# Output projection of a decoder layer: one Strassen scheme against two, one inside the other

## Chip, cores and metric

One Trainium2 chip, one of its cores. The metric is the device time of the whole kernel in microseconds (us). The kernel computes in fp32, with bf16 for the quantised cross attention and a split into two halves for the down projection.

## The reference, cut to what matters

Two batch entries of 512 tokens and 1024 features pass one decoder layer: self attention with a window of 128, a cross attention of quantised products, and a gated feed-forward, each followed by a layer norm.

```python
q = (x @ wq.T).reshape(B, N, N_Q, HD)...        # 32 heads of 128
k = (x @ wk.T)...; v = (x @ wv.T)...            # 8 heads of 128, each for 4 query heads
o = _gqa_swa_attention(q, k, v, SLIDE)
o = o.transpose(0, 2, 1, 3).reshape(B, N, N_Q * HD)
return o @ wo.T                                  # the output projection: 512 x 4096 by 4096 x 1024
...
x = _layernorm(x + _L0_attn_ref(x, L0_attn_wq, L0_attn_wk, L0_attn_wv, L0_attn_wo), axis=-1)
x = _layernorm(x + _L0_xattn_ref(x, ctx_4096, ...), axis=-1)
x = _layernorm(x + _L0_ffn_ref(x, L0_ffn_w_gate, L0_ffn_w_up, L0_ffn_w_down), axis=-1)
```

## The kernel before

The large products use Strassen's scheme: a product of two by two blocks is made from seven block products in place of eight, with sums of blocks formed beforehand on each side and sums of products formed afterwards.

Attention (`attention`) runs over 16 groups: batch entry `b` 0 and 1, and within each the 8 key heads `g`. For each group the queries, keys and values are projected (`project`, which calls `strassen`, line L113 for its matmuls): three calls with seven products each, a product being four matmuls of 128x256. For each of the four query tiles `i` of a group, `scores` multiplies queries by keys (L306) into `ps`, two PSUM banks; ACT copies the parts of the window to `s` (L318 to L322), VectorE lays the masked diagonal over them (L323), and the softmax follows. `weigh` transposes the weights (`pt`, L343) and multiplies by the values (`o`, L366 to L369), with a PSUM bank of its own. After the last tile `keep` (L379 on) forms the Strassen left sums of the group, four VectorE operations on 512 columns, and writes seven factors to `kept` in DRAM with five DMAs.

`project_out` multiplies these by the weights `wo`. One level of Strassen: for each of two token parts `q`, the seven products `k` in the order 1, 6, 2, 7, 5, 4, 3, and for each the 8 groups `s`. A step loads one left factor (128 KB) and one right factor (512 KB), three steps ahead, and issues two matmuls of 128x512 (L465). Products 2, 7, 4 and 3 go on accumulating in the banks of earlier ones. After the last group of a product, VectorE adds it to the residual `x` (L472). The sums of the right side are formed once, during attention, by `sum_output_weights` (L938 to L941), and lie in `wo_sums`.

`Cross` holds the cross attention: `context` quantises the context, `tokens` handles one tile of 128 tokens after another. `feed_forward` runs 22 units per batch entry, 21 of them a Strassen product of gate and up weights, and sums two or four units at a time in the down projection (`down`, L719).

Nothing of this runs one after the other. `Background` holds generators, and each call of `between` from the attention loop (six per query tile) or after each product of the feed-forward takes a step of them. `behind` holds the context of the first entry, then `output(0)`, then `output(1)`; `aside` holds the tokens of the cross attention; `ahead` holds the weight sums. `output(0)` starts with the second entry's attention. `output(1)` starts when the tokens of entry 0 are done, and runs mostly under the feed-forward of entry 0. A scheduler then sets the order of the instructions on each engine, save where `keep_in_program_order` holds one in place; each engine runs its own in order.

PSUM has eight banks. In attention: two for `ps_p` (Strassen and the cross attention), two for `ps_y` (the output of entry 0; Strassen uses them too as long as `b` is 0), two for the scores, one for transposes and one for `o`. In the feed-forward: two for `ps_p` (the output of entry 1 and the cross attention), four for Strassen (`ps_gu`, `ps_hu`), two for the down projection. With one pair of banks `strassen` reuses a bank after each other product; with two pairs it is "roomy" and has four to go round.

## Time and profile before

| | us |
|---|---|
| median of 3 runs | 1941.29 |
| lowest and highest | 1940.63, 1943.84 |
| the profiled execution's own time | 1941.39 |
| its span in the profile | 1939.6 |
| TensorE busy | 1913.4 |
| VectorE busy | 1130.0 |
| ACT busy | 545.5 |

The span is what the profile covers of the execution. Busy time of an engine is the part of the span in which it has an instruction in work. An fp32 matmul is two rows of the profile[...], so counts on TensorE are twice those of the code. The mean length of a matmul in the profile reaches from its start to the modelled end of its pipeline and overlaps the next one; the pace at which matmuls follow each other is read from their starts. "PEld" is the load of a matmul's stationary operand.

### The profile page before, as it was taken

Reading aid. Unit: us, or ns where it says so; the run is one execution under the profiler, and the core shown is the slowest. Engines: PE = TensorE matmul, PEld = TensorE weight load, DVE = VectorE, ACT = ScalarE, POOL = GpSimd, SP = SyncE. Lnnn points to the kernel's source line nnn. Section 1 sums busy time; section 2 is a strip of 40 time slices with the busy share of each in tenths; the row PEclk is TensorE's granted clock in tenths of the full one; section 3 lists DMA queues with packets and bytes.
Section 4 is the critical chain, followed back from the end, with each engine's and each line's share of the span. In section 5 each row is a group of like instructions: output and inputs, shape, how many; then the busy total and the mean of one; then the engine's idle time right before and its main releaser. Section 6 shows DMA issues by size and latency. Waiting matters only on the chain.

```text
span 1939.6 us, 22612 instructions
## 1 busy us (share of the span) xinstructions
PE 1913.4 (99%) x7986; PEld 1426.0 (74%) x7996; DVE 1130.0 (58%) x2316; ACT 545.5 (28%) x1547; POOL 13.7 (1%) x32
## 2 busy tenths in 40 slices
PE   9999999999999999999999999999999999999997
PEld 6888887887666666667866666666677878888885
DVE  4667787675344444537754545345458697555656
ACT  1333333332111222223333111111123254222224
POOL 0000000000000000000000000000000000000000
PEclk9999999999999999999999999999999999999999
DMA  8577786668888878785498877876754245443421
GB/s 314 167 235 256 239 271 218 234 235 272 272 273 285 264 265 278 258 273 197 173 311 286 276 258 262 282 259 200 253 187 135 94 168 199 171 168 137 140 88 44
DMA packets 242545, 431.44 MB, mean 222 GB/s; under 512 B 18560, under 2 KB 152960, under 8 KB 242432
## 3 DMA queue, kind: packets, MB, share of 16 engines
q1 hardware_dynamic: 240992, 427.63, 65.8%
q10 hardware_dynamic: 1440, 2.36, 0.4%
q8 instruction: 64, 1.05, 0.2%
q14 instruction: 49, 0.40, 0.1%
...
## 4 chain that ended last, share of the span: by engine, by line
PE 87%; DVE 6%; DMA 5%; ACT 2%; issue 1%; SPq 0%; DVEq 0%; ACTq 0%
PE prod L113 47%; PE y L465 19%; PE d L719 7%; PE ps L306 3%; DMA wd<-in_wd_dram 3%; PE o L368 2%; PE o L369 2%; PE pt L343 1%; PE m L595 1%; PE first L246 1%; DVE lo L676 1%; PE o L366 1%; ACT hi L675 0%; DMA or<-wo_sums 0%; PE x L603 0%
## 5 line engine op out<-in xcount | busy, mean ns | idle before, releaser
L465 PE MATMUL y<-or,ol 128*128 128x512 f32 x896 | 420.5, 592 | 1.3 <-DMA ol<-kept 0.5
L465 PEld LDWEIGHTS y<-or,ol 128*128 128x128 f32 x896 | 169.4, 190 | 125.1 <-issue 111.5
L113 PE MATMUL prod<-xT,w 128*128 128x256 f32 x752 | 178.9, 379 | 0.2 <-ACT a1T L589 0.2
L113 PE MATMUL prod<-t,w 128*128 128x256 f32 x752 | 175.7, 379 | 0.0
L113 PE MATMUL prod<-t,s 128*128 128x256 f32 x752 | 175.7, 379 | 0.0
L113 PEld LDWEIGHTS prod<-t,w 128*128 128x128 f32 x752 | 141.5, 190 | 36.3 <-issue 17.5
L113 PEld LDWEIGHTS prod<-t,s 128*128 128x128 f32 x752 | 141.7, 190 | 33.9 <-issue 12.9
L113 PEld LDWEIGHTS prod<-xT,w 128*128 128x128 f32 x752 | 140.6, 190 | 30.5 <-issue 12.7
L113 PE MATMUL prod<-x2T,wgu 128*128 128x256 f32 x672 | 160.8, 379 | 0.3 <-ACT g L133 0.3
L113 PE MATMUL prod<-t,sgu 128*128 128x256 f32 x672 | 156.2, 380 | 0.1
L113 PE MATMUL prod<-t,wgu 128*128 128x256 f32 x672 | 155.8, 379 | 0.0
L113 PEld LDWEIGHTS prod<-x2T,wgu 128*128 128x128 f32 x672 | 127.4, 190 | 30.9 <-issue 14.4
L113 PEld LDWEIGHTS prod<-t,sgu 128*128 128x128 f32 x672 | 127.1, 190 | 30.7 <-issue 13.2
L113 PEld LDWEIGHTS prod<-t,wgu 128*128 128x128 f32 x672 | 127.5, 190 | 29.5 <-issue 12.9
L136 DVE TENSOR_TENSOR st<-prod,st 128x256 f32<-128x256 f32 x89 | 37.6, 422 | 141.5 <-PE prod L113 141.3
L331 ACT ACTIVATE s<-s,top 128x128 f32<-128x128 f32 x256 | 99.5, 391 | 42.4 <-DVE top L328 42.3
L719 PE MATMUL d<-hi,act 128*128 128x512 f32 x256 | 108.9, 425 | 1.5 <-DVE acc L731 1.3
L733 DVE TENSOR_TENSOR acc<-d,acc 128x512 f32<-128x512 f32 x104 | 71.7, 691 | 59.6 <-PE d L719 59.1
L719 PE MATMUL d<-lo,act 128*128 128x512 f32 x256 | 101.2, 395 | 0.0
L113 PE MATMUL prod<-xT,s 128*128 128x256 f32 x376 | 89.6, 380 | 0.0
L675 ACT CAST hi<-wd 128x1024 fp32r<-128x1024 f32 x38 | 39.8, 1047 | 168.1 <-DMA wd<-in_wd_dram 95.8
L113 PE MATMUL prod<-x2T,sgu 128*128 128x256 f32 x336 | 80.1, 381 | 5.1 <-DVE u L139 5.1
...
## 6 DMA issues: line engine op xcount, KB each, us to landing
or<-wo_sums SPq DMA_DIRECT2D x128, 512.0 KB, 4.8
...
ol<-kept SPq DMA_DIRECT2D x224, 128.0 KB, 3.9
...
```

The costliest lines, as they stand in the source:

```text
L113: nc.tensor.matmul(ps, left[k - 1][:, c, :], right[k - 1][:, c, :], start=start and c == 0, stop=c == KH - 1, skip_group_check=True)
L136: nc.vector.tensor_tensor(u3, two, p1, ALU.add)
L246: nc.tensor.matmul(ps[h][:, part], weights[0][:, h, c], x0[:, c, part], start=c == 0 and k == 0, stop=c == KC - 1, skip_group_check=True,)
L306: nc.tensor.matmul(ps[:, c, cut // BLOCK : G + 1].rearrange("p d w -> p (d w)"), qT[b, g][:, G * i + c].rearrange("p h w -> p (h w)"), kT[ ...
L331: nc.scalar.activation(s[:, h, :], s[:, h, :], AF.Exp, bias=top[:, h : h + 1], scale=QSCALE, accum_out=total[:, h : h + 1],)
L343: nc.tensor.transpose(ps[:, :, ts(c, BLOCK)], s[:, c, :], ident)
L368: nc.tensor.matmul(ps, v[b, g][:, i - 1, :], both, start=True, stop=False)
L369: nc.tensor.matmul(ps, vd[b, g][:, i - 1, :], cur, start=False, stop=True)
L465: nc.tensor.matmul(ps, left[:, c], right[:, c], start=k in (1, 6, 5) and s == 0 and c == 0, stop=s == LAST and c == 1, skip_group_check=True,)
L675: nc.scalar.copy(hi, raw[u])
L719: nc.tensor.matmul(ps, act[:, ts(i, P)], half[:, ts(e, HALF)], start=start and k == 0, stop=stop and k == len(parts) - 1)
L733: nc.vector.tensor_tensor(acc[t][:, ts(e, HALF)], ps, acc[t][:, ts(e, HALF)], ALU.add)
```

## The change

The output projection applies the scheme twice, one inside the other: the seven products of the outer level are each made from seven quarter products, 49 in all, each a matmul of 128x256 per group. A step is now one outer product `k` and one group `g`, 56 for each batch entry. Its seven quarter products grow side by side in four PSUM banks, two to a bank in three of them. The outer products 2, 7, 4 and 3 go on accumulating on what is in the banks, as before. After the last group of each outer product `read` forms the inner level's sums and adds them to the blocks of the residual in which this stage of the outer accumulation counts. `gap` leaves four or two turns of the background free after it.

`keep` now works after every second tile: it forms the inner sums for the two blocks of a half, and after the second half also the outer sums of all seven, in one SBUF tile `factors`; 49 blocks go to DRAM. The inner sums on the right side are formed on the way by `right_sums`, one step ahead, from the outer factor that the step loads. Loads run two steps ahead, a left load being 448 KB.

The four banks `ps_y` are held through the whole kernel. The scores go in two pairs of blocks through one bank, with a turn of other work between the pairs; `o` shares the bank of the transposes; and Strassen in the feed-forward has only the two banks of `ps_p` for entry 0, and two of `ps_p` with the four of `ps_y` for entry 1. The room for the weight sums is taken from other pools, and their steps go on at the faster rate through the second entry's attention too. The tokens of the cross attention follow in the order in which the residual is ready, 2, 3, 0, 1, after the weight sums, with more turns.

```diff
+HQ = HALF // 2
+SLOT = {1: 0, 2: 1, 3: 6, 4: 3, 5: 4, 6: 5, 7: 2}
...
         ps_t = ctx.enter_context(tc.tile_pool(name="ps_t", bufs=1, space=PSUM))
-        ps_o = ctx.enter_context(tc.tile_pool(name="ps_o", bufs=1, space=PSUM))
+        factors = ctx.enter_context(tc.tile_pool(name="a_factors", bufs=1)).tile([P, 7, 7, P], F32, tag="factors", name="factors")
...
-        def scores(b, g, i):
+        def scores(b, g, i, meanwhile):
             s = work.tile([P, G, P], F32, tag="s", name=f"s_{b}_{g}_{i}")
-            ps = ps_s.tile([P, G, 2 * P // BLOCK, BLOCK], F32, tag="s", name=f"ps_{b}_{g}_{i}")
...
             if i == 0:
                 nc.gpsimd.memset(s, MASKED)
+            for pair in range(G // 2):
+                ps = ps_s.tile([P, 2, 2 * P // BLOCK, BLOCK], F32, tag="s", name=f"ps_{b}_{g}_{i}_{pair}")
+                for k in range(2):
+                    c = 2 * pair + k
+                    at = i * P + c * BLOCK
+                    cut = max(P - at, 0)
+                    nc.tensor.matmul(
+                        ps[:, k, cut // BLOCK : G + 1].rearrange("p d w -> p (d w)"),
+                        qT[b, g][:, G * i + c].rearrange("p h w -> p (h w)"),
+                        kT[b, g][:, at - P + cut : at + BLOCK], start=True, stop=True,
+                    )
+                for k in range(2):
+                    c = 2 * pair + k
+                    if i:
+                        nc.scalar.copy(s[:, c, c * BLOCK :], ps[:, k, : G - c].rearrange("p d w -> p (d w)"))
+                    if c:
+                        nc.scalar.copy(s[:, c, : c * BLOCK], ps[:, k, G - c : G].rearrange("p d w -> p (d w)"))
+                mixed = s.rearrange("p c (k w) -> p (c k) w", w=BLOCK)[:, 10 * pair : 10 * pair + 6 : 5]
+                nc.vector.copy_predicated(
+                    mixed, mask_i.unsqueeze(1).to_broadcast([P, 2, BLOCK]), ps[:, :, G]
+                )
+                if pair == 0:
+                    meanwhile()
...
-            ps = ps_o.tile([P, G, P], F32, tag="o", name=f"o_{b}_{g}_{i}")
+            ps = ps_t.tile([P, G, P], F32, tag="t", name=f"o_{b}_{g}_{i}")
...
-            if place == 0:
-                outputs[b, g, half] = work.tile([P, 2, 2, NH], F32, tag=f"oT{half}", name=f"oT_{b}_{g}_{half}", bufs=2 - half)
-            nc.scalar.copy(outputs[b, g, half][:, :, :, ts(place, P)], ps.rearrange("p (k j) t -> p k j t", k=2))
...
+            nc.scalar.copy(factors[:, 2 * half : 2 * half + 2, 2 * place : 2 * place + 2],
+                           ps.rearrange("p (k j) t -> p k j t", k=2))
+            if place:
+                keep(b, g, half)
+            if i == TPB - 1 and g == NKV - 1:
+                complete.add(b)
+        def left_sums(a11, a12, a21, a22, s1, s2, s4):
+            tc.keep_in_program_order(nc.vector.tensor_tensor(s1, a21, a22, ALU.add))
             nc.vector.tensor_tensor(s2, s1, a11, ALU.subtract)
             nc.vector.tensor_tensor(a21, a11, a21, ALU.subtract)
             nc.vector.tensor_tensor(s4, a12, s2, ALU.subtract)
...
+        def keep(b, g, half):
+            own = slice(2 * half, 2 * half + 2)
+            left_sums(*(factors[:, own, k] for k in range(7)))
+            if half:
+                left_sums(*(factors[:, k] for k in range(7)))
+            for k in (3, 4, 5, 2, 6) if half else (0, 1):
+                nc.sync.dma_start(out=kept[b][:, g, k], in_=factors[:, k])
...
-                for _ in range(STEPS - 1):
+                def other():
                     next(rest, None)
                     between(b, g, i)
+                s = scores(b, g, i, other)
+                weigh(pending, other)
+                pending = b, g, i, s
+                for _ in range(STEPS - 2):
+                    other()
...
-def project_out(nc, b, xres, spaces, psum, kept, complete, wo_d, sums, x_d):
+def project_out(nc, tc, b, xres, spaces, psum, kept, complete, wo_d, sums, x_d, gap):
...
     respool, stream, work = spaces
     LAST = NKV - 1
+    grow = {1: (True, ((0, 1), (1, 0), (1, 1))), 2: (False, ((0, 0),)), 6: (True, ((0, 1),)),
+            7: (False, ((1, 1),)), 4: (False, ((1, 0),)), 5: (True, ((1, 1),)), 3: (False, ((0, 1),))}
+    steps = [(k, g) for k in grow for g in range(NKV)]
+    AHEAD = 2
+    loaded, rights = {}, {}
     def load(n):
         if n >= len(steps):
             return
+        k, g = steps[n]
+        left = stream.tile([P, 7, P], F32, tag="left", name=f"ol_{b}_{n}")
+        nc.sync.dma_start(out=left, in_=kept[:, g, SLOT[k]])
+        right = stream.tile([P, 2, 2, HQ], F32, tag="right", name=f"or_{b}_{n}")
         src = wo_d[(0, 2, 3)[k - 1]] if k <= 3 else sums[:, k - 4]
+        nc.sync.dma_start(out=right.rearrange("p j e c -> p j (e c)"), in_=src[:, g])
         loaded[n] = left, right
+    def right_sums(n):
+        if n >= len(steps):
+            yield
+            return
+        right = loaded[n][1]
+        b11, b12, b21, b22 = (right[:, j, e] for j in range(2) for e in range(2))
+        t = stream.tile([P, 3, HQ], F32, tag="sums", name=f"ot_{b}_{n}", bufs=2)
+        t1, t2, t4 = (t[:, j] for j in range(3))
+        tc.keep_in_program_order(nc.vector.tensor_tensor(t1, b12, b11, ALU.subtract))
+        nc.vector.tensor_tensor(t2, b22, t1, ALU.subtract)
+        yield
+        tc.keep_in_program_order(nc.vector.tensor_tensor(b12, b22, b12, ALU.subtract))
+        nc.vector.tensor_tensor(t4, b21, t2, ALU.subtract)
+        rights[n] = dict(zip(range(1, 8), (b11, b21, b22, t4, t1, t2, b12)))
+        yield
     while b and (b - 1, "tokens") not in complete:
         yield
     for i in range(TPB):
         nc.sync.dma_start(out=x[:, i], in_=x_d[ts(b * TPB + i, P), :])
         xres[b * TPB + i] = x[:, i]
+    for _ in right_sums(0):
+        yield
+    banks = [psum.tile([P, 2, HQ], F32, tag="p", name=f"y{k}_{b}") for k in range(4)]
+    places = {1: (0, 0), 6: (0, 1), 7: (1, 0), 2: (2, 0), 3: (2, 1), 4: (3, 0), 5: (3, 1)}
+    order = list(places)
+    def read(k):
+        w = work.tile([P, 4, HQ], F32, tag="y", name=f"yw_{b}_{k}")
+        p1, u4, u2, u3 = (w[:, j] for j in range(4))
+        q1, q6, q7, q5 = banks[0][:, 0], banks[0][:, 1], banks[1][:, 0], banks[3][:, 1]
+        add = lambda out, in0, in1: nc.vector.tensor_tensor(out, in0, in1, ALU.add)
+        nc.scalar.copy(p1, q1)
+        tc.keep_in_program_order(add(u2, q6, p1))
+        add(u3, q7, u2)
+        add(u4, q5, u2)
+        rows = w[:, 0:2], u3.unsqueeze(1).to_broadcast([P, 2, HQ])
+        grown = banks[2], banks[3]
+        to = [[x[:, 2 * h + q, ts(e, HALF)].rearrange("p (e c) -> p e c", e=2) for q in range(2)] for h, e in grow[k][1]]
+        if len(to) == 1:
+            for q in range(2):
+                add(to[0][q], grown[q], to[0][q])
+            for q in range(2):
+                add(to[0][q], rows[q], to[0][q])
+        else:
+            whole = w[:, 0:2], w[:, 2:4]
+            for q in range(2):
+                add(whole[q], grown[q], rows[q])
+            for block in to:
+                for q in range(2):
+                    add(block[q], whole[q], block[q])
+    for n, (k, g) in enumerate(steps):
+        while n + AHEAD < len(steps) and steps[n + AHEAD][1] == LAST and b not in complete:
             yield
         load(n + AHEAD)
+        left, mine = loaded.pop(n)[0], rights.pop(n)
+        following = right_sums(n + 1)
+        for part in (order[:4], order[4:]):
+            for j in part:
+                bank, half = places[j]
+                nc.tensor.matmul(
+                    banks[bank][:, half], left[:, SLOT[j]], mine[j],
+                    start=grow[k][0] and g == 0 and half == 0, stop=g == LAST, skip_group_check=True,
+                )
+            next(following, None)
+            if g == LAST and part[-1] == order[-1]:
+                read(k)
+                if k in (5, 3):
+                    complete.add((b, 1 if k == 5 else 0))
+                for _ in range(gap):
+                    yield
+            yield
...
-        for i in (0, 2, 1, 3):
-            while (b, i % 2) not in complete:
...
     with ExitStack() as ctx:
         accp = ctx.enter_context(tc.tile_pool(name="c_acc", bufs=1))
         work = ctx.enter_context(tc.tile_pool(name="c_work", bufs=2))
-        inter = ctx.enter_context(tc.tile_pool(name="c_inter", bufs=5))
+        inter = ctx.enter_context(tc.tile_pool(name="c_inter", bufs=3))
         wdp = ctx.enter_context(tc.tile_pool(name="c_wd", bufs=3))
...
-                for k, _ in enumerate(strassen(nc, (ps_gu, ps_hu), work, left.pop(u), right[b], outs, u)):
+                for k, _ in enumerate(strassen(nc, (ps_p, ps_y if b else ps_p), work, left.pop(u), right[b], outs, u)):
...
     spill = {t: scratch.tile([P, D], F32, tag=f"spill{t}", name=f"spill{t}") for t in range(TPB)}
-    kept = [scratch.tile([P, 7, NKV, 2, NH], F32, tag=f"kept{b}", name=f"kept{b}") for b in range(B)]
+    kept = [scratch.tile([P, NKV, 7, 7, P], F32, tag=f"kept{b}", name=f"kept{b}") for b in range(B)]
+    ps_y = ctx.enter_context(tc.tile_pool(name="ps_y", bufs=4, space=PSUM))
...
-    def output(b, psum):
-        return project_out(nc, b, xres, (resid, stream, y_work), psum, kept[b], complete, wo, wo_sums, x)
+    def output(b):
+        return project_out(nc, tc, b, xres, (resid, stream, y_work), ps_y, kept[b], complete, wo, wo_sums, x, 2 if b else 4)
     def cross_tokens(b):
+        while ahead.queue:
+            yield
...
+    def weights_room(in_first):
+        return (stream, "right") if in_first else (pools[1], "raw")
...
+        for n, (g, j, q) in enumerate(steps):
+            pool, tag = weights_room(in_first[0])
+            w = pool.tile([P, 4, Q4], F32, tag=tag, name=f"wo_{g}_{j}_{q}")
             nc.sync.dma_start(out=w, in_=wo[:, :, g, j, ts(q, Q4)].rearrange("k p e -> p k e"))
+            yield
             b11, b12, b21, b22 = (w[:, k] for k in range(4))
...
         if (b, g, i, place) == (0, 2, 0, 1):
             behind.add(cross.context(0), 5)
+        if (b, g, i, place) == (1, 0, 0, 1):
+            in_first[0] = False
         if (b, g, i, place) == (1, 0, 1, 1):
-            behind.add(output(0, ps_y))
-            behind.add(output(1, pools[3]))
+            behind.add(output(0))
+            behind.add(output(1))
             aside.add(cross_tokens(0))
         behind.step()
-        if place == 0:
+        if place in (0, 2, 4) if b else place == 0:
             aside.step()
-            if b and g == NKV - 1:
-                prepare_feed_forward()
-        if (place == 0 and (b or g or i)) or (place == 3 and b == 0 and i % 2):
+        if place == 0 and b and g == NKV - 1:
+            prepare_feed_forward()
+        if (place == 0 and (b or g or i)) or (place == 3 and i % 2):
             ahead.step()
...
     def in_feed_forward(k):
-        if k in (1, 5):
+        if k in (1, 3, 5):
             aside.step()
         behind.step()
```

## The prediction

> **What bounds the kernel now.** I read the page from the top: busy time, the slices, then the chain that ended last, then the groups of the lines that the change replaces, and last the busy time by stage.
>
> ```profile
> PE 1913.4 (99%) x7986; PEld 1426.0 (74%) x7996; DVE 1130.0 (58%) x2316; ACT 545.5 (28%) x1547; POOL 13.7 (1%) x32
> ...
> PE   9999999999999999999999999999999999999997
> PEld 6888887887666666667866666666677878888885
> DVE  4667787675344444537754545345458697555656
> ...
> PE 87%; DVE 6%; DMA 5%; ACT 2%; issue 1%; SPq 0%; DVEq 0%; ACTq 0%
> ...
> L465 PE MATMUL y<-or,ol 128*128 128x512 f32 x896 | 420.5, 592 | 1.3 <-DMA ol<-kept 0.5
> L465 PEld LDWEIGHTS y<-or,ol 128*128 128x128 f32 x896 | 169.4, 190 | 125.1 <-issue 111.5
> L113 PE MATMUL prod<-t,w 128*128 128x256 f32 x752 | 175.7, 379 | 0.0
> L113 PEld LDWEIGHTS prod<-t,w 128*128 128x128 f32 x752 | 141.5, 190 | 36.3 <-issue 17.5
> ```
>
> TensorE is busy 99% of the span, in every slice but the last, and the chain is TensorE for 87%. So the time is the sum of TensorE's instructions plus 1939.6 - 1913.4 = 26.2 us of gaps. The output projection (L465) is 420.5 us of that busy time. Each fp32 matmul shows as two rows: the code has 448 of these matmuls and the page 896.
>
> A busy span ends later than the moment at which the next matmul can start, so for a sum I need the pace. The chain of waits, in order of time, gives it where the two shapes alternate:
>
> ```profile
> 1047.58 1.73 PE prod L113 x8
> 1049.31 1.72 PE y L465 x4
> 1051.02 1.73 PE prod L113 x8
> 1052.75 1.72 PE y L465 x4
> ```
>
> Eight rows of 128x256 take 1.73 us, 0.216 each; four of 128x512 take 1.72, 0.430 each. The stretch has no gap.
>
> The stages: tokens of the first batch entry go through attention up to about 430 us; attention of the second runs with the first output projection to 990; then the feed-forward of the first runs with the second output projection to 1460; then the feed-forward of the second.
>
> ```profile
> 20.00:430.00 410.00, 408.70 (x1960) 340.89 (x1960) 292.31 (x676) 135.77 (x560) 3.68 (x7) 1.00 0.71 240
> 430.00:990.00 560.00, 559.21 (x2234) 386.24 (x2237) 282.00 (x639) 149.22 (x547) 4.20 (x8) 1.00 0.78 255
> 1040.00:1460.00 420.00, 418.46 (x1548) 282.42 (x1551) 210.54 (x370) 86.22 (x129) 0.00 (x0) 1.00 0.75 250
> ```
>
> Columns: the stretch, then busy us of PE, PEld, DVE, ACT, POOL, the granted clock, DMA share, GB/s. TensorE loses 1 to 2 us in each. VectorE is at 71%, 50% and 50%: the first row shows that at 71% it still costs TensorE nothing.
>
> **TensorE: what goes and what comes.** Removed: 896 rows of 128x512, 896 x 0.430 = 385 us. Added: 2 batch entries x 56 steps x 7 quarter products = 784 matmuls of 128x256, 1568 rows, priced by L113, which has the same shape, type and a fresh weight load for each: 1568 x 0.216 = 339 us. Difference -46 us. It all lies on the path, since TensorE is the path.
>
> Here a rule speaks against the change. There are 672 more weight loads, and L113 shows each at 190 ns against a pace of 216. The Trainium skill (TensorE: Matmul & The Clock Gate, Part 3, "What overlaps and what doesn't") says that a weight load overlaps a matmul in flight only when it goes to another group of rows of the array; here all go to the whole array. By that rule 672 loads would stand bare, +128 us, and the sum would be +82. The row decides: 190 ns of load and 256 columns fit into 0.216 us in 4,984 rows of L113, so the load is hidden. I take -46.
>
> **VectorE.** Dense pace, from the timeline's starts:
>
> ```profile
> 254.06 0.42 DVE L939 TENSOR_TENSOR wo_sum<-wo,wo_sum 128x256 f32<-128x256 f32 x1
> 254.39 0.42 DVE L940 TENSOR_TENSOR wo<-wo 128x256 f32<-128x256 f32 x1
> 254.73 0.42 DVE L941 TENSOR_TENSOR wo_sum<-wo,wo_sum 128x256 f32<-128x256 f32 x1
> ...
> 284.56 0.68 DVE L94 TENSOR_TENSOR s<-s,w 128x512 f32<-128x512 f32 x1
> 285.15 0.69 DVE L95 TENSOR_TENSOR w<-w 128x512 f32<-128x512 f32 x1
> ```
>
> That is 0.335 us for 256 columns and 0.60 for 512, so about 1.00 for 896 (estimate along that line). Added: right-hand sums 112 steps x 4 = 448 of 256 columns; left sums, in place of 4 of 512 a group, 8 of 256 and 4 of 896 (16 groups); reading the seven products, 14 times, 42 of 256 and 64 of 512 in place of 36 of 512. Together 618 x 0.335 - 36 x 0.60 + 64 x 1.00 = 207 - 22 + 64 = 249. The mask becomes 128 half-size copies for 64 whole ones, about +6. So VectorE goes from 1130 to about 1385, 73% of the new span. By stage: first attention +34 for left sums and 3 for masks, 329 of 405 us (81%); second attention +34 +75 +15 +3, 409 of about 537 (76%); first feed-forward +75 +15, 300 of about 397 (76%). It stays off the path on average, but all its waiting is in one queue, and evictions of PSUM stand in it.
>
> **ACT, DMA, SP, POOL.** ACT's score copies stay at 7 a tile; 14 copies of p1 at 256 columns (0.37) replace 4 of 512: +3 us on an engine at 28%. DMA: 112 loads of 512 KB for 224 (-59 MB), left loads 112 x 448 KB for 224 x 128 KB (+22), kept writes 49 for 28 quarter blocks of 64 KB a group (+22): -15 MB, and in runs of 3.5 KB where the left loads had 512 B. SP issues 112 loads fewer on each of two tiles and 32 more writes: about -190 issues of 0.37 to 0.47 us. What can turn late: a step's right side must be there a step earlier, for VectorE sums it one step ahead. A step is 7 x 0.432 = 3.0 us plus two Strassen products of 1.73 = 6.5 us; the landing is 4.8 to 5.1 us at the median. Behind a late one stand all PSUM evictions. It covers itself by 1.4 us; I leave it at nothing and keep it in the range. POOL's queue is not moved past.
>
> **New waits on TensorE**, each bounded from both sides.
> - Scores now come as two pairs of blocks through one bank. The second pair waits for three ACT copies (0.27 + 0.30 + 0.20) and the mask (about 0.25), 1.0 us, and what stands before the mask on VectorE; in between lies a product of 1.73 us. 64 times, between 0 and 0.5 us: 0 to 32. Nearest row: L323 sat idle before it for 3.9 us in all, so the mask seldom waits. I take 4.
> - Evictions behind the fuller VectorE, with two banks in place of four for Strassen in the first feed-forward. Both halves have a row: two banks at VectorE 50% lost 0.8 us (430 to 990), four banks at 71% lost 1.3. The pair at 76% has none: 0 to 40, I take 6.
> - The last units of the first feed-forward: the second output ends about four units before the end (129 turns at 7 a unit; the order shows its last product in unit 16 of 21), and the rest runs in two banks with a single product of 1.73 us between uses of a bank, against 0.35 + 0.42 for latency and add, and 0.69 for each activation step in front. 21 switches, 0 to 0.7 us: I take 4.
> - The end of the first stage with both projections: head group 7 has only the first six output steps (18 us) as filler where it had 14 steps of 1.72 (24 us), and the order has nothing but one o between the last score pair and its transposes. The chain from there is copies 0.75, mask 0.25, maximum 0.7, scale 0.2, four exponentials 2.3, reciprocal 0.2, product 0.7 = 5.1 us, less 1.7 for o: 3.4, about as much again over the tile before it and the load of the first left block behind. 0 to 16, I take 8.
> - Tokens of the first entry fall closer together, in group 6: 0 to 8, I take 3.
> - Reading the seven products: the next product writes into the same banks. The Trainium skill (PSUM — Partial Sum Buffer, "PSUM bank collisions raise a hardware error") wants accesses kept apart by bank and not by address, so no half can restart while its neighbour is read. The read needs 0.37 + 3 x 0.42 + 2 x 0.69 = 3.0 us; bare, 14 times, that is 42 us and the gain is gone. The four or two turns left free after it put 6.9 or 3.5 us of Strassen in between, so I take 1 (0 to 15).
>
> Sum of the middles: 4 + 6 + 4 + 8 + 3 + 1 = 26 us. Net: -46 + 26 = -20. The profiled execution took 1941.4 us (span 1939.6 and 1.8 around it), and the median of the runs is 1941.3, so the two can be used alike: 1921.
>
> **Rivals.**
> - The whole gain: the order hides every wait. For it: TensorE lost 1 to 2 us a stage in spite of a VectorE at 71%. Then 1941 - 46 = 1895, with up to 12 us of waits 1907. Against it: each of six places gets thinner at once.
> - Slower: the second output's stage becomes bound by evictions. Place: first feed-forward, 21 units x 7 products, two banks shared with the cross attention's tiles. For it: VectorE goes from 50% to 76% there and its queue is in order; four right-hand sums (1.3 us), five to nine additions of a read, or three quantising steps (2.2 us) can stand before an eviction. Price: 147 evictions x the wait beyond cover. It decides from (46 - 20) / 147 = 0.18 us a product if the other waits stay as above; at 0.4 us it costs 59, and the time is 1941 - 46 + 20 + 59 = 1974. Against: from 430 to 990 the same two banks held, and the output steps between products give 0.9 to 1.7 us more cover.
> - The scores' single bank, above all in the first attention, where VectorE is at 81% and no output steps lie between: at 0.7 us a pair 64 x 0.7 = 45 us in place of the 4 that I have counted: 1941 - 46 + 22 + 45 = 1962.
> - That it doesn't save work: excluded as far as rows can do it. The added matmuls are counted, and L113 prices their very shape.
>
> **How the numbers follow.** Waits of 12 to 40 us, 1907 to 1935: 0.49. Nearly the whole gain, below 1907: 0.22. Small gain, 1935 to 1937: 0.02; within 0.2% (about 4 us, what a measurement of this kernel can tell from no change), 1937 to 1945: 0.03. Slower: evictions in the feed-forward 0.13, scores' bank or late right sides 0.11. So faster 0.73, same 0.03, slower 0.24. The range leaves out about 0.05 below 1895 and 0.12 above 1956; the likeliest case alone is 1907 to 1935.
>
> **What would show each step.** In the profile after: y in 1568 rows of 128x256 and a pace of 0.216 in the chain; VectorE near 1385; right-hand sums with little idle time released by DMA; TensorE idle about 52 us in all, with the new gaps near the end of the second attention and in the last units of the first feed-forward. I am wrong if TensorE's idle time stands spread over the first attention (scores' bank) or over the whole first feed-forward (evictions), or if the y rows run slower than 0.216.

## The result: slower by 0.8%, and the profile after

The changed kernel takes 1958.4 us at the median of six runs (1950.2 to 1961.7); the kernel before took 1941.0 beside it. The ratio is 1.0082, with a 95% interval of 1.0058 to 1.0106: slower by 11 to 21 us, where 20 us less were predicted. The profiled execution took 1958.5 us, its span is 1956.7.

The page after, the lines that answer to those of before: busy time, three engines in forty slices, the chain by engine, and the groups of the output projection and of the reference product.

```profile
PE 1891.6 (97%) x8658; PEld 1554.2 (79%) x8668; DVE 1385.5 (71%) x3026; ACT 551.5 (28%) x1553; POOL 13.7 (1%) x32
...
PE   9999999999999999999898999999998999999997
...
DVE  4678888878567677767777776666777688555656
...
PE 47%; DVE 14%; DMA 8%; ACT 3%; issue 2%; SPq 0%; DVEq 0%; ACTq 0%
...
L521 PE MATMUL y<-or,ol 128*128 128x256 f32 x896 | 250.4, 382 | 7.6 <-DVE or L466 5.8
L521 PEld LDWEIGHTS y<-or,ol 128*128 128x128 f32 x896 | 168.0, 190 | 38.3 <-DVE or L466 12.0
L521 PE MATMUL y<-ot,ol 128*128 128x256 f32 x672 | 183.2, 380 | 6.4 <-DVE ot L464 6.4
```

The new matmuls are there, 896 + 672 = 1568 rows, with a weight load of 190 ns each. TensorE's busy time fell by 21.8 us only, three slices lost their 9, and the chain, which was TensorE for 87%, is TensorE for 47% and VectorE for 14% (the shares shown add up to 74% only, so it is a hint and not a sum). The output rows now wait for VectorE's right-hand sums (L464, L466).

The pace of the new rows, from the chain of waits in order of time (start, length, row, count):

```profile
566.49 1.73 PE y L521 x8
...
569.94 1.73 PE prod L117 x8
```

Eight y rows take as long as eight rows of the reference product, 0.216 us a row, as predicted. So the time didn't go into the new matmuls. To see where it went, I took each group of TensorE's rows in the timeline and subtracted from the distance between its start and the next group's start its rows at full pace (0.216 us for 256 fp32 columns, in proportion for others, at least 0.108). What is left is loss: waits, their tails, and rows at a slower clock. This splits each span in two; another price for the rows of other shapes moves both losses together, by up to 15 us, and their difference by about 1.

| | rows at full pace | loss | span |
|---|---|---|---|
| before | 1912.3 | 27.3 | 1939.6 |
| after | 1864.9 | 91.8 | 1956.7 |

The work fell by 47.4 us, the loss grew by 64.5, and the span by the difference, 17.1. By stretches of the span (us of loss; in the other kernels below the same work lies up to 50 us earlier, in two up to 70 later):

| kernel | 0-400 | 400-700 | 700-900 | 900-1200 | 1200-1400 | 1400-1600 | later | sum |
|---|---|---|---|---|---|---|---|---|
| before | 6.7 | 0.9 | 2.1 | 5.6 | 1.0 | 1.9 | 9.1 | 27.3 |
| after | 8.5 | 19.2 | 5.9 | 31.2 | 0.2 | 18.8 | 8.0 | 91.8 |

The first attention lost next to nothing new, though it has the fullest VectorE. Three stretches carry the loss: the start of the first output projection, the end of the attention with the start of the second projection, and the end of the first feed-forward. The busy time by stage says the same (stretch, length, busy us of PE, PEld, DVE, ACT, POOL, granted clock, DMA share, GB/s); first before, then after:

```profile
400.00:700.00 300.00, 300.00 (x1175) 207.14 (x1174) 140.83 (x316) 71.00 (x286) 2.10 (x4) 1.00 0.82 268
...
900.00:1200.00 300.00, 297.44 (x1164) 205.00 (x1165) 163.50 (x320) 83.23 (x243) 1.05 (x2) 1.00 0.77 261
...
1400.00:1600.00 200.00, 199.49 (x879) 155.19 (x881) 146.09 (x276) 72.06 (x106) 1.94 (x3) 1.00 0.45 153
```

```profile
0.00:400.00 400.00, 394.93 (x1845) 322.06 (x1847) 304.46 (x712) 132.92 (x519) 5.63 (x18) 1.00 0.76 259
400.00:700.00 300.00, 287.57 (x1340) 239.36 (x1339) 218.58 (x524) 68.32 (x283) 2.10 (x4) 0.99 0.78 265
...
900.00:1200.00 300.00, 281.15 (x1283) 225.53 (x1286) 221.70 (x480) 89.11 (x227) 1.05 (x2) 0.98 0.65 225
1200.00:1400.00 200.00, 200.00 (x912) 170.76 (x911) 128.83 (x263) 30.89 (x53) 0.00 (x0) 1.00 0.62 213
1400.00:1600.00 200.00, 189.99 (x843) 147.62 (x846) 146.39 (x289) 58.73 (x90) 1.93 (x3) 0.97 0.36 121
```

VectorE is at 76% in the first row and TensorE loses 1.8 us more there than before; at 73% in the second row it loses 18.3 more. From 1400 to 1600 VectorE is busy for 146 us before and after alike, and the loss grew from 1.9 to 18.8. At 64% (1200 to 1400) with only two banks there is next to no loss, 0.2 us. The share of VectorE alone doesn't tell these stages apart, so I looked at which instructions stand in front of which. Two places, read in the timeline. First, 402 to 409 us, VectorE, then TensorE:

```profile
402.18 1.08 DVE L388 TENSOR_TENSOR factors<-factors 128x896 f32<-128x896 f32 x1
403.18 0.68 DVE L97 TENSOR_TENSOR s<-w 128x512 f32<-128x512 f32 x1
403.78 1.08 DVE L389 TENSOR_TENSOR factors<-factors 128x896 f32<-128x896 f32 x1
404.78 1.08 DVE L390 TENSOR_TENSOR factors<-factors 128x896 f32<-128x896 f32 x1
405.78 1.08 DVE L391 TENSOR_TENSOR factors<-factors 128x896 f32<-128x896 f32 x1
...
408.59 0.42 DVE L154 TENSOR_TENSOR vT<-prod,st 128x256 f32<-128x256 f32 x1
```

```profile
409.06 0.75 PE L117 MATMUL prod<-xT,w 128*128 128x256 f32 x2 [4.14 <-DVE vT L154]
```

The eviction L154, 0.42 us of work, stands behind the four wide left-hand sums of a head group (L388 to L391) and the sums of a weight tile (L97 to L100), and TensorE waits 4.1 us for its bank. Its product was done at 403.0 us; three of the wide sums and the four of the weight tile, 5.4 us, went first from then on. Before the change the left-hand sums of the same group took 2.5 us, the weight tile's stood there too, and TensorE didn't wait:

```profile
399.04 0.69 DVE L384 TENSOR_TENSOR oS<-oT 128x512 f32<-128x512 f32 x1
...
400.97 0.68 DVE L387 TENSOR_TENSOR oS<-oT,oS 128x512 f32<-128x512 f32 x1
401.57 0.42 DVE L136 TENSOR_TENSOR st<-prod,st 128x256 f32<-128x256 f32 x1
```

Second, 522 to 533 us in the changed kernel, the two engines again:

```profile
522.16 0.41 DVE L491 TENSOR_TENSOR yw<-y,yw 128x256 f32<-128x256 f32 x1
524.66 0.43 DVE L1002 TENSOR_TENSOR sum<-raw 128x256 f32<-128x256 f32 x1 [2.08 <-DMA raw<-in_wgu_dram]
...
528.00 3.69 DVE L491 TENSOR_TENSOR xres<-yw,xres 128x512 f32<-128x512 f32 x6
...
532.87 0.41 DVE L129 TENSOR_TENSOR st<-prod,st 128x256 f32<-128x256 f32 x1
```

```profile
533.34 1.99 PE L117 MATMUL prod<-t,w 128*128 128x256 f32 x8 [2.60 <-DVE st L129]
```

Here VectorE itself waits 2.1 us for the load of a weight tile whose sums it is to form (L1002), then reads seven products (L491), and the eviction L129 comes behind all of it: TensorE waits 2.6 us. The read's six additions to the residual alone, 3.69 us, are longer than that wait. Loads of right factors came late as well: VectorE stood idle before L463, the first right-hand sum of a step, for 18.6 us in 11 steps until a right factor had landed, and before L1002 for 14.3 us in 9.

Each long wait costs again. After the wait of 4.1 us the granted clock (the column behind the five engines) is at half:

```profile
408.00:409.00 1.00, 0.00 (x0) 0.00 (x0) 1.00 (x4) 0.00 (x0) 0.00 (x0) 1.00 1.03 419
...
410.00:411.00 1.00, 1.00 (x5) 1.00 (x5) 1.00 (x4) 0.00 (x0) 0.00 (x0) 0.50 0.92 375
...
412.00:413.00 1.00, 1.00 (x6) 0.91 (x5) 0.77 (x2) 0.23 (x1) 0.00 (x0) 0.50 1.01 288
```

The trace shows five such stretches before the end of the work, of 3.4 or 6.8 us, 23.9 us in all; at half the pace that is about 12 of the 64.5 us (an estimate). The kernel before had none. These rows count as busy, which is one reason why busy time fell by 22 us where the work fell by 47.

### The profile page after: what moved, and what is told of

Read it like the earlier page. It is cut to its first block, busy times and chain, and to the rows that moved or that the text cites. A ratio compares the mean times of both kernels' runs of the same rounds, so it can differ in the third digit from the quotient of the medians.

```text
span 1956.7 us, 24498 instructions
## 1 busy us (share of the span) xinstructions
PE 1891.6 (97%) x8658; PEld 1554.2 (79%) x8668; DVE 1385.5 (71%) x3026; ACT 551.5 (28%) x1553; POOL 13.7 (1%) x32
## 4 chain that ended last, share of the span: by engine, by line
PE 47%; DVE 14%; DMA 8%; ACT 3%; issue 2%; SPq 0%; DVEq 0%; ACTq 0%
PE prod L117 24%; PE y L521 11%; PE d L758 7%; DMA wd<-in_wd_dram 3%; DMA raw<-in_wgu_dram 2%; DMA sums<-raw 1%; DVE lo L715 1%; DMA or<-in_wo_dram 1%; PE ps L317 1%; PE m L636 1%; DMA or<-wo_sums 1%; PE o L376 1%; PE o L377 1%; ACT s L341 1%; DVE xres L491 1%
## 5 line engine op out<-in xcount | busy, mean ns | idle before, releaser
L521 PE MATMUL y<-or,ol 128*128 128x256 f32 x896 | 250.4, 382 | 7.6 <-DVE or L466 5.8
L521 PE MATMUL y<-ot,ol 128*128 128x256 f32 x672 | 183.2, 380 | 6.4 <-DVE ot L464 6.4
L117 PE MATMUL prod<-xT,w 128*128 128x256 f32 x752 | 183.2, 382 | 5.0 <-DVE vT L154 4.1
L117 PE MATMUL prod<-t,s 128*128 128x256 f32 x752 | 180.0, 380 | 0.7 <-ACT kT L137 0.5
L521 PEld LDWEIGHTS y<-ot,ol 128*128 128x128 f32 x672 | 126.4, 190 | 27.6 <-DVE ot L464 8.6
L117 PEld LDWEIGHTS prod<-t,sgu 128*128 128x128 f32 x672 | 128.6, 192 | 20.2 <-ACT a1T L630 1.3
L327 ACT COPY s<-ps 128x128 f32<-128x128 f32 x192 | 39.6, 232 | 265.0 <-PE ps L317 265.0
```

Of the source, the lines that this page charges most:

```text
L117: nc.tensor.matmul(ps, left[k - 1][:, c, :], right[k - 1][:, c, :], start=start and c == 0, stop=c == KH - 1, skip_group_check=True)
L327: nc.scalar.copy(s[:, c, c * BLOCK :], ps[:, k, : G - c].rearrange("p d w -> p (d w)"))
L521: nc.tensor.matmul(banks[bank][:, half], left[:, SLOT[j]], mine[j], start=grow[k][0] and g == 0 and half == 0, stop=g == LAST, skip_group_ ...
```

## The experiments

All ratios are to the kernel before, measured on the same chip in the same comparison; "us" behind a ratio is the ratio's difference from 1 times 1940. The changed kernel stands at +16 (11 to 21) on that scale, so a difference between it and another run is good to some 5 us. The losses of all, by the method above:

| kernel | 0-400 | 400-700 | 700-900 | 900-1200 | 1200-1400 | 1400-1600 | later | sum |
|---|---|---|---|---|---|---|---|---|
| e1 before, late tokens | 6.2 | 0.8 | 2.4 | 6.9 | 0.5 | 2.3 | 7.9 | 27.0 |
| e2 early rows | 8.6 | 21.7 | 3.8 | 28.6 | 1.6 | 16.1 | 7.0 | 87.4 |
| e3 weight sums slower | 8.8 | 11.9 | 4.9 | 57.4 | 0.3 | 16.5 | 9.1 | 108.9 |
| e4 no right sums | 9.6 | 10.0 | 2.0 | 9.5 | 1.7 | 16.1 | 6.9 | 55.8 |
| e5 four banks late | 8.2 | 16.1 | 5.9 | 28.7 | 0.3 | 11.5 | 10.6 | 81.3 |
| e6 weight sums first | 13.1 | 12.0 | 4.3 | 32.4 | 0.3 | 16.9 | 9.4 | 88.4 |
| e7 left sums spread | 9.3 | 16.6 | 4.7 | 31.2 | 0.3 | 17.2 | 10.3 | 89.6 |
| e8 four mends | 13.1 | 12.7 | 2.6 | 30.7 | 1.6 | 11.3 | 10.4 | 82.4 |
| e9 before, more load | 6.4 | 5.6 | 3.8 | 5.7 | 4.3 | 3.8 | 8.3 | 37.9 |
| e10 sums unused | 8.5 | 14.5 | 4.2 | 21.5 | 1.4 | 13.8 | 9.4 | 73.3 |
| e11 right sums on GpSimd | 9.5 | 28.1 | 5.8 | 22.5 | 2.2 | 16.6 | 8.4 | 93.1 |
| e12 the same, three mends | 14.7 | 15.2 | 6.6 | 19.0 | 4.6 | 10.3 | 10.8 | 81.2 |
| e13 no left sums | 7.7 | 8.3 | 7.0 | 20.0 | 0.9 | 17.3 | 10.8 | 72.0 |
| e14 no sums, four banks | 7.3 | 2.8 | 2.3 | 3.7 | 1.1 | 11.1 | 9.2 | 37.5 |
| e15 second only | 11.6 | 4.4 | 2.4 | 19.7 | 1.4 | 9.5 | 10.0 | 59.0 |
| e16 second only, slower tokens | 10.2 | 4.7 | 2.9 | 20.2 | 1.0 | 2.2 | 9.8 | 51.0 |
| e17 left sums on GpSimd | 53.3 | 40.1 | 14.0 | 37.0 | 1.0 | 1.9 | 14.0 | 161.3 |
| e18 second only, GpSimd | 11.5 | 18.7 | 17.8 | 38.0 | 1.5 | 2.0 | 10.5 | 100.0 |

My first theory was that the tokens are the cause: the residual now becomes complete only with the last two of seven outer products, so the tokens come late and close together, and two of the three losing stretches are where they are. The rival was VectorE's extra work.

**e1: the kernel before, with late tokens alone.**

```diff
-            while (b, i % 2) not in complete:
+            while not {(b, 0), (b, 1)} <= complete:
...
-        if place == 0:
+        if place in (0, 3) if b else place == 0:
             aside.step()
...
-        if k in (1, 5):
+        if k in (1, 3, 5):
```

> The kernel before, with one thing of the change alone: the tokens of the cross attention may not start on the first column half of the output, but only when both halves of the output projection are done, and then take two turns a tile in place of one (three a unit in the feed-forward). In the changed kernel TensorE loses about 20 us more than before from 940 to 1060 us and 17 us more from 1400 to 1600, which is where the tokens are there. Theory (late tokens: their chains of layer norm, quantising and transposes stand in TensorE's queue with too little else to do): this kernel is slower than before by 8 to 30 us, 1949 to 1971, with the loss in those two stretches. Rival (VectorE's extra work, not the lateness, is the cause): with VectorE at 58% late tokens cost nothing, 1939 to 1944.

Measured: 1.0009 (0.9995 to 1.0023), +2 us; loss 27.0 against 27.3. The tokens ran at 879 to 990 us and from 1436 on, as late as in the changed kernel, and cost nothing. The theory fell, as far as lateness alone is concerned.

**e2: the changed kernel, with earlier tokens.** The outer products in another order complete the first row half after five of seven.

```diff
-    grow = {1: ..., 2: ..., 6: ..., 7: ..., 4: ..., 5: ..., 3: ...}
+    grow = {1: ..., 2: ..., 5: ..., 3: ..., 6: ..., 7: ..., 4: ...}
...
-        for i in (2, 3, 0, 1):
+        for i in (0, 1, 2, 3):
```

> The changed kernel with its outer products in the order 1, 2, 5, 3, 6, 7, 4: the first row half of the output is complete after five of seven products, about 100 us earlier, and its two tokens start then; the rest is the same work. Theory (late tokens): the losses at 940 to 1060 and 1400 to 1600, 35 us more than before, fall by a third to a half; 1958 less 10 to 18, so 1940 to 1948. Rival (VectorE's fuller queue): the same additions stand in the queue, and the time stays at 1954 to 1960.

Measured: 1.0076 (1.0048 to 1.0103), +15 us, not told apart from the change. Two of four tokens moved ahead by 30 to 70 us; 900 to 1200 lost 28.6 in place of 31.2. It came out as the rival said.

**e3 and e6: the weight sums.** Both take sums of gate and up weights out of the second attention, where their late loads hold VectorE; e3 lets them end later, e6 has more of them in the first attention.

```diff
-        if (place == 0 and (b or g or i)) or (place == 3 and i % 2):
+        if (place == 0 and (b or g or i)) or (place == 3 and b == 0 and i % 2):     # e3
+        if (place == 0 and (b or g or i)) or (place == 3 and b == 0):               # e6
             ahead.step()
```

> The changed kernel with the sums of the gate and up weights taken once a tile in the second attention, as in the first half of their way, and not up to twice. In the changed kernel the chain from 500 to 560 us runs through loads into the one buffer of these sums, with the right-hand sums behind them in VectorE's queue, and TensorE loses 7 us there. Theory (VectorE stands in front of a load that is late, and the right-hand sums wait behind it): 4 to 8 us less, 1950 to 1954. Rival (the load of additions, not the wait in front of them): the additions are the same, 1956 to 1960. The tokens of the first entry wait for the last of these sums, so a later end of them could give some of it back.

> The changed kernel with the sums of the gate and up weights taken twice every tile in the first attention (not every other tile) and once a tile in the second: they end some three head groups earlier, so no token waits for them, and few stand in front of the right-hand sums. Theory (late loads of these sums in VectorE's queue cost the 7 us at 500 to 560 us): 4 to 9 us less than the changed kernel, 1949 to 1954, and the earlier try's loss by late tokens doesn't come. Rival (VectorE's load): the first attention goes from 76% to 82% busy on VectorE and begins to lose; 1956 to 1965.

Measured: e3 1.0206 (1.0180 to 1.0233), +40 us, beyond both of its expectations; e6 1.0079 (1.0064 to 1.0094), +15, as its rival said. In both the 19.2 us of 400 to 700 fell to 12, so the sums behind late loads did cost 7 there. e6 gave it back: its first attention lost 13.1 in place of 8.5, and the wait for L154 at 410 grew to 5.5 us. In e3 the tokens had to wait for the last weight sums (a line of the change) and ran at 978 to 1051, partly after the end of the attention: 900 to 1200 lost 57.4, 26 more than the change. So late tokens cost nothing in e1, and 26 us in e3, where they come later still and there is less other work beside them.

**e5: four banks for the last units of the first feed-forward.**

```diff
-                ... strassen(nc, (ps_p, ps_y if b else ps_p), work, left.pop(u), right[b], outs, u)
+                ... strassen(nc, (ps_p, ps_y if b or finished() else ps_p), work, left.pop(u), right[b], outs, u)
```

> The changed kernel, but in the first feed-forward Strassen's products take the four output banks from the unit on in which the second output projection is done (the last units, where the tokens of the second entry are), in place of sharing two banks with the tokens. The changed kernel loses 17 us more than before from 1400 to 1600 us. Theory (the two shared banks make the tokens' chains block the products): 10 to 15 us of them go, 1943 to 1949. Rival (the tokens' layer norm stands in VectorE's queue, whatever the banks): the waits on the normalised rows, 3.2 and 2.1 us, stay, and less than 5 us go: 1953 to 1959.

Measured: 1.0051 (1.0036 to 1.0066), +10 us. Of 18.8 us in 1400 to 1600, 7 went: between the two expectations. Of the rest, 2.1 us are a token's transposes waiting for its layer norm and 2.1 a product waiting for a load of factors; most of it went with the tokens' pace of e16 below.

**e7: left-hand sums one a turn.** A list holds the four wide sums of a group and each turn of the background puts out one.

```diff
+                    if later:
+                        later.pop(0)()
                     next(rest, None)
                     between(b, g, i)
```

> The changed kernel with the four wide left-hand sums (896 columns, 1.0 us each) of a finished head group put out one a turn in place of all four in one turn. At 405 us they stand, with the sums of the second entry's x, in front of one eviction, and TensorE waits 4.1 us and then runs 3.4 us at half clock; at 540 and 1053 us they stand before right-hand sums. Theory (a burst in an in-order queue): 4 to 9 us go, 1949 to 1954. Rival (the same total of additions, so the same waits): 1956 to 1960.

Measured: 1.0083 (1.0068 to 1.0098), +16 us: nothing. It settles nothing either, because the order in the queue hardly changed. At this place the four wide sums still all stand ahead of L154, mixed with those of the weight tile (which the expectation took for sums of x). Two of them, from VectorE's timeline of e7:

```profile
404.86 1.08 DVE L409 TENSOR_TENSOR factors<-factors 128x896 f32<-128x896 f32 x1
405.86 1.08 DVE L420 TENSOR_TENSOR factors<-factors 128x896 f32<-128x896 f32 x1
...
409.67 0.41 DVE L154 TENSOR_TENSOR vT<-prod,st 128x256 f32<-128x256 f32 x1
```

**e8: the mends of e2, e5, e6 and e7 together.**

> The changed kernel with four mends at once: outer products in the order 1, 2, 5, 3, 6, 7, 4; four banks for the last units of the first feed-forward; weight sums done earlier; left-hand sums one a turn. Theory (the losses of single places add up): about 2 + 12 + 6 + 6 = 26 us less than the changed kernel, 1928 to 1938, faster than before by 0.2 to 0.6%. Rival (VectorE's load sets the sum, and a wait mended here comes back there): 1945 to 1955.

Measured: 1.0046 (1.0028 to 1.0064), +9 us, about what e5 gives alone. The number is the rival's. That a wait comes back elsewhere is seen for the weight sums alone (0 to 400 lost 13.1 in place of 8.5, as in e6); the mends of e2 and e7 had brought nothing by themselves.

**e4, e10 and e9: the right-hand sums, their use, and their load.** In e4 the sums are gone, in e10 they are formed and not used, and e9 lays their load on the kernel before.

```diff
-        tc.keep_in_program_order(nc.vector.tensor_tensor(t1, b12, b11, ALU.subtract))       # e4
-        nc.vector.tensor_tensor(t2, b22, t1, ALU.subtract)
...
-        rights[n] = dict(zip(range(1, 8), (b11, b21, b22, t4, t1, t2, b12)))                # e4, e10
+        rights[n] = dict(zip(range(1, 8), (b11, b21, b22, b21, b11, b22, b12)))
```

```diff
         left, right = loaded.pop(n)                                                         # e9
+        spare = work.tile([P, HALF // 2], F32, tag="spare", name=f"spare_{b}_{n}")
+        for c in range(2):
+            nc.vector.tensor_tensor(spare, right[:, c, : HALF // 2], right[:, c, HALF // 2 :], ALU.subtract)
```

> The changed kernel without the four right-hand sums of an output step (the products read the loaded blocks in their place, so that part of the computation is left out): 448 additions, about 150 us of VectorE, and the waits of the products on them go; VectorE's busy time falls from 1385 to about 1235. Theory of two causes: what falls away is the loss at the output steps, 560 to 940 and 1060 to 1200 and a part of 400 to 560, about 15 to 20 us of 64; the late tokens stay with some 30 us: 1936 to 1944. Rival (VectorE's load is the whole cause): nearly all 64 us of loss go but those of before, 1900 to 1915. Rival (right-hand sums cost nothing by themselves): 1954 to 1960.

> The changed kernel in which the four right-hand sums of a step are formed as before into their own tile, but the products read the loaded blocks (the sums' use is left out): the same load on VectorE, 1385 us busy, without the products' wait for it. The kernel without these sums at all took about 1926 where the changed one takes 1957. Theory (the wait of the products): near the kernel without sums, 1926 to 1936. Rival (the load itself): near the changed kernel, 1948 to 1958.

> The kernel before with 448 more additions of 256 columns on VectorE, two in each of its 224 output steps, from the step's loaded block into a spare tile that nobody reads: the load of the changed kernel's right-hand sums (about 150 us, VectorE 1130 to 1280) without a product that waits for them. Theory (the sums cost because products stand behind them, in a queue that is in order): the load alone costs little, 0 to 6 us, 1940 to 1947. Rival (VectorE's load alone, through evictions that come later): 12 to 30 us, 1953 to 1971.

Measured: e4 0.9940 (0.9920 to 0.9960), -12 us; e10 1.0014 (1.0000 to 1.0029), +3; e9 1.0081 (1.0054 to 1.0108), +16. So the right-hand sums cost 27 to 28 us of time: 14 by standing in the queue (e10 less e4), 13 because products wait for them (the change less e10), each good to some 5 or 6 us. e4 and e10 fell between their expectations. e9's time is its rival's, where my theory had 0 to 6 us. Its profiled execution took 1951 us, at the lower end of its runs, with 10.6 us more loss; the largest part, 4.9 us of waits (1.2 before), is TensorE's value products waiting for the copies behind their transposes. But e9 is not the load alone, as it was meant to be. VectorE's waits in e9 (total us, times, longest):

```profile
DVE spare L455 <- DMA or<-wo_sums: 132.2, 80, 5.4
DVE spare L455 <- DMA or<-in_wo_dram: 85.4, 61, 4.5
```

For 218 us VectorE stands idle in front of an addition whose block hasn't landed, and all that is behind it in its queue stands too. In e10 that is 39.9 us in 19 places, in the changed kernel 18.6. A loaded block is also held until VectorE has read it. So what stands in the queue can cost by its length, by the load it waits for and by the buffer it holds, and no run separates the three.

**e13 and e14: the left-hand sums, and everything at once.**

```diff
-            left_sums(*(factors[:, own, k] for k in range(7)))
-            if half:
-                left_sums(*(factors[:, k] for k in range(7)))
```

> The changed kernel without the left-hand sums of a finished head group (the slots of the sums hold zeros, so that part of the computation is left out): 8 additions of 256 columns and 4 of 896 in each of 16 groups, about 107 us of VectorE, and its busy time falls from 1385 to about 1280. Theory (these sums cost at the few places where they stand in front of an eviction or a right-hand sum): the 4.1 us wait at 405 us with its half clock and the waits at 533 and 1053 us go, and some of the load: 10 to 20 us less than the changed kernel, 1938 to 1948. Rival (only the right-hand sums matter): 1953 to 1960.

> The changed kernel without left-hand and without right-hand sums (both left out of the computation), and with four banks for the last units of the first feed-forward: VectorE at about 1125, as before the change. Theory (sums on VectorE and the two shared banks are all of the added loss): TensorE's losses return to the 27 us of before, and the time is that of the whole gain, 1895 to 1905. Rival (a third cause: tokens that come late, the scores' pairs in one bank, or fewer output steps at the end of the attention): 1910 to 1925.

Measured: e13 0.9979 (0.9967 to 0.9991), -4 us, so the left-hand sums cost 20, as the theory said; e14 0.9824 (0.9807 to 0.9840), -34 us, 1905.8 at the median, 0.8 us above its theory's range and below its rival's. The page of e14:

```profile
PE 1872.1 (98%) x8658; PEld 1550.5 (81%) x8668; DVE 1123.4 (59%) x2386; ACT 545.3 (29%) x1549; POOL 17.3 (1%) x34
```

This closes the account within the noise. The three parts add up nearly as if they were independent: 27 + 20 + 6 = 53 us by the single runs, 50 together. With VectorE back where it was before the change, the losses are 37.5 us; up to 1400 us they are those of before (17.2 against 16.3), although the tokens are still late, the scores still go in pairs through one bank, and the end of the attention still has only six output steps. What is left, 11.1 in 1400 to 1600, holds a wait of 2.3 us for a load of factors with the half clock behind it, and one of 2.1 us of a token's transposes for its layer norm. Both kinds went with the slower pace of e16 below; in e14 itself that wasn't tried.

**e15 and e16: the new scheme for the second projection alone.** The first projection keeps one level (its code of before, with two blocks loaded ahead); e16 also gives tokens two turns a unit.

```diff
+        if b == 0:
+            return project_one(nc, b, xres, (resid, stream, y_work), ps_y, kept[b], complete, wo, wo_sums, x)
...
-        if k in (1, 3, 5):                                                                  # e16
+        if k in (1, 5):
             aside.step()
```

> The first output projection as before (seven products of 512 columns, its head groups' four sums of 512), the second as in the changed kernel, with the products' order 1, 2, 5, 3, 6, 7, 4, four banks for the last units, weight sums done in the first attention, and the first entry's tokens once a tile as before. TensorE's work falls by half of 46, 23 us. Theory (the added sums cost while VectorE has the softmax beside them, and are free in the feed-forward, where the changed kernel lost 0.2 us from 1200 to 1400): losses as before up to 940 us, some 12 us more after it: 1941 - 23 + 12 = 1930, between 1924 and 1937, faster than before. Rival (the start of the second output, the end of the attention and the tokens of the second entry cost as much as the half gain): 1938 to 1950.

> The same, with the second entry's tokens taking two turns a unit in the feed-forward, as before, and not three. Theory (a token's transposes wait in TensorE's queue for its layer norm, 2 to 3 us each, because the next turn comes too soon): 2 to 6 us less than with three turns. Rival (later tokens move the wait to the end of the first feed-forward): 0 to 5 us more.

Measured: e15 1.0051 (1.0036 to 1.0066), +10 us, as its rival said; e16 1.0010 (1.0001 to 1.0020), +2. The slower pace is worth 8 us, and 1400 to 1600 fell from 9.5 to 2.2: with three turns a token's transposes stood in TensorE's queue 2.1 us before its layer norm was done, and other waits beside them went too. In e16 losses up to 900 us are as before but for 3.5 in the first attention (where the weight sums come earlier, as in e6) and 3.8 from 400 to 700. The half gain of 24 us is lost at 900 to 1200 (20.2 against 5.6) and by these. There the left-hand sums of a group stand again in front of what TensorE waits for (TensorE's, then VectorE's rows of e16):

```profile
1014.54 2.08 PE L374 MATMUL o<-cur,v 128*128 128x512 f32 x2 [3.54 <-DVE cur L356]
...
1055.69 0.70 PE L547 MATMUL y<-ot,ol 128*128 128x256 f32 x2 [2.68 <-DVE ot L490]
```

```profile
1012.20 1.09 DVE L417 TENSOR_TENSOR factors<-factors 128x896 f32<-128x896 f32 x1
...
1013.80 0.68 DVE L356 COPY cur<-pt 128x512 f32<-128x512 f32 x1
...
1053.28 1.08 DVE L417 TENSOR_TENSOR factors<-factors 128x896 f32<-128x896 f32 x1
...
1055.22 0.42 DVE L490 TENSOR_TENSOR ot<-or,ot 128x256 f32<-128x256 f32 x1
```

**e11, e12, e17 and e18: sums on GpSimd.** GpSimd is 1% busy. e11 puts the right-hand sums there, e12 adds the mends of e2, e5 and e6; e17 puts the left-hand sums there (but the last group's), with these mends and the tokens' pace of e16; e18 does so in e16.

```diff
-        tc.keep_in_program_order(nc.vector.tensor_tensor(t1, b12, b11, ALU.subtract))       # e11, e12
+        tc.keep_in_program_order(nc.gpsimd.tensor_tensor(t1, b12, b11, ALU.subtract))
...
+            engine = nc.vector if b and g == NKV - 1 else nc.gpsimd                         # e17, e18
+            left_sums(engine, *(factors[:, own, k] for k in range(7)))
```

> The changed kernel with the right-hand sums of the output steps on GpSimd, which is 1% busy, in place of VectorE. If GpSimd needs less than some 1.5 us an addition, four fit into a step of 6.5 us, and neither evictions nor sums stand behind each other. Theory (one in-order queue serves both): the time falls to what the kernel without the sums showed, 1926 to 1936. Rival (GpSimd is too slow for a step, or slows VectorE while both run): the y rows wait for the sums at every step, 1960 to 2100.

> The same, with three other mends: four banks for the last units of the first feed-forward, weight sums done earlier, outer products in the order 1, 2, 5, 3, 6, 7, 4. Theory: the gains add up, some 8 us below the kernel with GpSimd alone, 1918 to 1928, faster than before by 0.6 to 1.1%. Rival: as with GpSimd alone, slower.

> The changed kernel with the left-hand sums on GpSimd (but those of the last head group of the second entry, which stay on VectorE), and with four mends that the runs before point to: products in the order 1, 2, 5, 3, 6, 7, 4, four banks for the last units of the first feed-forward, the second entry's tokens two turns a unit, weight sums mostly in the first attention. An addition of 256 columns took GpSimd 0.86 us in the run with the right-hand sums there, and VectorE's busy time was some 66 us more than in the run without those sums, with as many of its instructions. Theory (bursts of left-hand sums in front of evictions cost more than their load): 18 us less by the left sums, 8 by the banks, 5 by the pace, 4 by the weight sums, some 6 of it lost again to GpSimd's presence: about 1930, 1924 to 1938, faster than before. Rival (GpSimd slows VectorE by as much as it takes off it): 1940 to 1950.

> The kernel with the second output projection alone in the new scheme and the slower tokens (about 1942, of which TensorE loses 16 us from 1000 to 1060), with the left-hand sums of the second entry on GpSimd but for the last head group. Theory (from 1006 to 1016 us the burst of eight of them stands in front of a mask, a maximum and the copy of the transposed scores): 6 to 10 us go, 1932 to 1936, faster than before by some 0.3%. Rival (the last head group's own burst at 1047 us and GpSimd's hold on VectorE weigh as much): 1939 to 1944.

Measured: e11 1.0108 (1.0078 to 1.0137), +21 us; e12 1.0033 (1.0016 to 1.0050), +6; e17 1.0477 (1.0459 to 1.0496), +93; e18 1.0267 (1.0251 to 1.0283), +52. e11 came out as its rival said, and e12 slower too, though by less; e17 and e18 lie far beyond both of their expectations. In e11 GpSimd is fast enough (0.88 us an addition; the products waited 5.8 us for its sums, in the changed kernel 12.2 for VectorE's), and VectorE is rid of the sums, but not of all their time. Compare the pages of e4, which has no right-hand sums, and of e11:

```profile
PE 1880.1 (98%) x8658; PEld 1554.2 (81%) x8668; DVE 1232.2 (64%) x2578; ACT 547.0 (28%) x1551; POOL 13.7 (1%) x32
```

```profile
PE 1895.7 (97%) x8668; PEld 1554.6 (79%) x8668; DVE 1298.5 (66%) x2578; ACT 547.2 (28%) x1551; POOL 399.5 (20%) x480
```

VectorE has 2578 instructions in both and takes 66 us longer beside GpSimd. e17 shows how (GpSimd's, then VectorE's timeline):

```profile
103.98 2.41 POOL L389 TENSOR_TENSOR factors<-factors 128x896 f32<-128x896 f32 x1
106.35 2.51 POOL L390 TENSOR_TENSOR factors<-factors 128x896 f32<-128x896 f32 x1
108.83 2.51 POOL L391 TENSOR_TENSOR factors<-factors 128x896 f32<-128x896 f32 x1
```

```profile
104.37 0.41 DVE L143 TENSOR_TENSOR vT<-prod,st 128x256 f32<-128x256 f32 x1
104.70 2.23 DVE L98 TENSOR_TENSOR s<-s,w 128x512 f32<-128x512 f32 x1
106.86 2.55 DVE L99 TENSOR_TENSOR w<-w 128x512 f32<-128x512 f32 x1
109.34 2.55 DVE L100 TENSOR_TENSOR s<-w,s 128x512 f32<-128x512 f32 x1
111.81 0.41 DVE L146 TENSOR_TENSOR vT<-prod,st 128x256 f32<-128x256 f32 x1
```

An addition of two SBUF tiles, 0.68 us elsewhere, takes 2.2 to 2.55, and each ends 0.55 us after the instruction that GpSimd had in work; an addition with one input from PSUM takes its usual 0.41. So a burst of 10 us on GpSimd becomes a burst on VectorE, and the mask behind it lets TensorE wait 5.7 us. Over the whole of e17 VectorE is busy for 1398.5 us, with 180 instructions fewer than the changed kernel and its 1385.5. In e18 a third queue joins in: SP issues the writes of the factors (L428), which wait for GpSimd, and the loads of the next output steps stand behind them:

```profile
631.83 9.16 SPq L428 DMA_DIRECT2D kept<-factors  x5
641.08 0.39 SPq L579 DMA_DIRECT2D ol<-kept  x1
641.51 0.67 SPq L582 DMA_DIRECT2D or<-wo_sums  x1
```

TensorE waited for such loads four times, 22 us in all. These runs don't answer whether it is the burst or the load of the left-hand sums that costs: on GpSimd they are still a burst. That stays open.

No kernel with the new scheme that does the whole computation was faster than before; the nearest is e16, which stays 0.2 to 4 us slower. The whole change with four late banks and the tokens' slower pace on VectorE was not tried; the single runs would put it at about +2 us (an estimate: 16 less 6 for the banks, less 8 for the pace).

## Why the prediction was wrong

- **TensorE's work, -46: right.** 1568 rows at 0.216; the rows at full pace fell by 47.4. The rule weighed there would have added 128 us for bare weight loads; 190 ns of load hide under 216 ns of pace in these rows too.
- **VectorE's sum, 1385: right to 0.5 us.** By stage it was near as well: 329, 409 and 300 us predicted, 323, 405 and 292 measured in the same stretches (20 to 430, 430 to 990, 1040 to 1460). So it wasn't the load that was misjudged, but its effect.
- **"It stays off the path on average, but all its waiting is in one queue": this is the step that failed.** I named the queue and then sized it by shares: "two banks at VectorE 50% lost 0.8 us, four banks at 71% lost 1.3 ... I take 6". Both rows came from mixes in which the left-hand sums of a group took 2.5 us. The 249 us that I added came as bursts of 5.3 us (left-hand sums, 4 x 0.335 + 4 x 1.00), as work that products wait for (right-hand sums), and behind loads. Left out, they give back 20 and 27 us, where the 6 stood (the places of the terms 8 and 3 below are among them). Whether the left-hand sums cost by coming in bursts or by their load stays open; for the right-hand sums about half comes of standing in the queue and half of products that wait for them.
- **Late right-hand sides, left at nothing: wrong, though described.** "Behind a late one stand all PSUM evictions" is what happened at 522 us; there the late load was that of a weight sum in a single buffer, whose faster rate in the second attention I had read in the diff and not costed. It took 7 us (e3, e6). The right sides themselves were late too, in 11 of 112 steps; behind two of these TensorE waited, 0.8 us at 1099 and 1.1 at 1148, and what the rest cost was not separated.
- **End of the attention 8 and tokens 3: 25.6 more were lost from 900 to 1200.** The place was right, the cause wasn't: with the same six output steps and the same late tokens, e14 lost 3.7 there. Without right-hand sums it was 9.5, without left-hand sums 20.0.
- **Last units of the first feed-forward, 4: 17.** The place and the banks were right, at 7 us; about as much again, measured from e15 to e16, is three turns a unit for the tokens, which I had counted as turns and not as an order in TensorE's queue.
- **Scores' second pair, 4: 1.2 us of waits for the mask, in three places.**
- **Reading seven products, 1: right for the wait that it priced**, the restart of a bank: 0.2 us of loss from 1200 to 1400, where products are read too (no run tests the rule on banks itself). It left out that a read is also a burst on VectorE, as at 528 us in front of L129.
- **Missing altogether: the half clock after a wait**, about 12 us, which turned waits of about 50 us into 64.
- **The rivals.** The slower one with the whole first feed-forward bound by evictions in two banks is refuted in its place (1200 to 1400). The scores' bank is refuted too. The slower time came from their common root, VectorE's queue, for the most part in places that neither named. The whole gain, 1895, was not reached even without the sums (1906).
